# A graph network on one core: other plans for the sparse products, matmuls issued in pairs of groups, pads left out of the first sorting steps, and the W_hh products made ahead

## The chip, the core and the metric

The kernel runs on one core of a Trainium2 chip. The core has a matrix engine (TensorE, PE in the profile; its weight loads are listed as PEld), a vector engine (VectorE, DVE), a scalar engine (ScalarE, ACT), a general engine (GpSimd, POOL) and a queue that only issues transfers (SyncE, SP). Each engine works through its own queue in order and waits on semaphores for the others. The metric is the time of one execution on the device in microseconds (us); a smaller number is better. Differences of 0.3% and less can't be told from no change here.

## The reference

There are N = 12500 nodes with H = 128 features, E = 200000 edges (src, dst) with 16 attributes and a type from 0 to 8. Four message layers follow each other. The first is a gated recurrent layer (GRU), and the other three are graph isomorphism layers (GIN) over the same edges in the other direction:

```
# layer 0: GRU
msg = x[src] @ W_msg.T + b_msg + edge_embed[type]
m   = segment_sum(msg, dst, N)
gi  = m @ W_ih.T + b_ih ;  gh = x @ W_hh.T + b_hh
r, z = sigmoid(gi_r + gh_r), sigmoid(gi_z + gh_z)
n   = tanh(gi_n + r * gh_n)
x   = layernorm(x + (1 - z) * n + z * x)
# layers 1 to 3: GIN, with self loops, ei[0] = src, ei[1] = dst
ee  = edge_attr @ enc_w + enc_b
agg = segment_sum(h[dst] (and ee beside or added), src, N)
h   = relu(bn(agg @ w1 + b1)) @ w2 + b2      (relu after layers 1 and 2)
out = layernorm(x + h)
```

## The kernel before

**Blocks and slots.** The nodes are cut into 98 blocks of 128. A message layer computes, for each of the 98 output blocks, the sum of the rows that its edges name. The edges of an output block come in two forms. For the first `ic` input blocks, the edges of each pair (output block, input block) have 32 slots (`SL`); four such pairs fill a *cell tile* of 128 slots. The edges to the remaining input blocks are packed without regard to their block into `rt` *row tiles* of 128 edges; the last `OV` places of the last row tile also take edges that don't fit into 32 slots. A `Plan` (L31 to 48) holds these numbers: plan C (layer 1) has `ic` = 72 and `rt` = 5, plan D (layers 2 and 3) has `ic` = 60 and `rt` = 7. Layer 0 has cells alone: 25 tiles for 98 blocks.

**One output block in `layer`.** The input table is kept on chip in bf16 as three pieces per number (`X`, 384 columns per block). A cell tile takes four matmuls with 32 columns of weights each (L1550): one-hot weights `g`, made from the row `inr`, pick 32 rows out of each of four input blocks into PSUM. Three tiles make a group (`TG`). ScalarE, in layer 0 for every other group together with VectorE, casts the group from PSUM into `e` (L1556, L1557, L1559). One matmul per tile with the one-hot weights `st` (s in the profile) then adds the 128 slots into the sums of the output block (`scatter`, L1507, the PSUM tile acc). A row tile needs no such step: GpSimd fetches its 128 rows from the table in memory with one indirect DMA (`fetch`, L1484, tile x), and one matmul adds them (`scatter_rows`, L1515). VectorE builds `g` (L1471) and `s` in four pieces (L1474) one block ahead. `finish` adds the three pieces of acc into `s` with three VectorE instructions (L1527 to L1529). Every two blocks a generator does the dense part: `gru` in layer 0 and `gin` in the others; it is advanced by `tick` once per group and yields between steps that wait for each other. All dense steps share one PSUM tile, d.

**Edge attributes.** The generator `attributes` (L729) sums each block's edge attributes. Per block, GpSimd issues 17 indirect DMAs (L736, tile eat), then `add_up` splits, builds one-hots and adds with 17 matmuls (L764). It is advanced during the second sort, in layer 0 (`pace`: k = 1 and 5, and k = 3 in four blocks of five) and in layer 1 (k = 3).

**Before the layers.** Two bitonic sorts of 128x2048 keys run on VectorE, B and then A (`sorter`; L316, L317, L321, L322); 1600 columns hold keys and the others hold pads. Keys are transposed on TensorE and copied back by ScalarE (`turn`). A histogram (`Sizes`, L548, L557, L567) is counted beside sort B. During sort A the kernel also does the attributes' first blocks, the weights (`load_weights`) and the first table (`first_table`). After it, the sorted keys go to memory, and GpSimd gathers the slots of layer 0 from there (`runs`, L791, tile cells); `Slots.decode` turns them into `inrow`, `outcol` and `typecol`.

**Order.** In the sorts the order of VectorE, ScalarE and TensorE is that of the program text (`manual_schedule`). In the layers a scheduler orders every engine's instructions by its own estimates of when each becomes ready.

## Time and profile before

Three runs took 5763.25 to 5779.61 us, with a median of 5772.15 us. The profiled execution took 5775.41 us; its span from the first to the last instruction is 5773.6 us.

| stage, us from the start of the span | length | PE busy | DVE busy | ACT busy | POOL busy | indirect DMAs for attributes (L736) and rows (L1484) |
|---|---|---|---|---|---|---|
| 572 to 1197, sort A and its end | 625 | 167.08 | 476.78 | 104.91 | 500.66 | 405 and 0 |
| 1279 to 2836, layer 0 | 1557 | 1411.98 | 1158.89 | 996.93 | 1073.81 | 935 and 0 |
| 2836 to 3949, layer 1 | 1113 | 999.81 | 492.97 | 739.88 | 821.18 | 323 and 499 |
| 3949 to 4874, layer 2 | 925 | 832.56 | 400.23 | 611.55 | 686.63 | 0 and 685 |
| 4874 to 5774, layer 3 | 900 | 827.81 | 428.78 | 579.76 | 674.90 | 0 and 680 |

The times of the stages' starts are those of the first matmul L1550 of a layer or of the first row fetch L1484 (layer 1). In the profile "busy" is the union of an engine's instructions. For GpSimd the issue of one indirect DMA counts as an instruction, and the time between two issues does not count as busy. In a line of the timeline, the first number is the start, the second the length, "x3" a run of three equal instructions, and the bracket says how long the engine had been idle and what ended that.

### The profile page before, as it was taken

What the parts mean: (1) busy time and instruction counts of PE and PEld (TensorE: products, weight loads), DVE (VectorE), ACT (ScalarE), POOL (GpSimd) and SP (SyncE); (2) the same over time, 40 slices, a digit from 0 to 9 for tenths busy, and PEclk for the clock granted to TensorE, in tenths of its full rate; (3) what the DMA queues carried; (4) which work ended last, traced back from release to release, by engine and by line L of the source; (5) the groups of instructions that cost most, each with busy time, mean ns of one, the idle gap of its engine ahead of it and who ended that gap; (6) DMA issues with size and microseconds to landing.
All of it is one profiled execution on the core that took longest, in us unless ns stands there. A gap on an engine that the chain in (4) does not pass through costs nothing. (4 is left out here: it accounts for less than half of the span.)

```text
span 5773.6 us, 117175 instructions
## 1 busy us (share of the span) xinstructions
PE 4590.5 (80%) x45358; PEld 2754.9 (48%) x45358; DVE 3500.1 (61%) x9502; ACT 3396.2 (59%) x4901; POOL 3855.7 (67%) x3716
## 2 busy tenths in 40 slices
PE   3874252118999999999799989988999997999998
PEld 3774122104444444444355555554555554555555
DVE  9987679837887777777444444443444443444444
ACT  7772131106666666666566666665666665666665
POOL 1001878866676767766677777775777776777776
PEclk9755555559999999999899999999999998999999
DMA  5101130012333333323444444445555555555554
GB/s 65 38 1 33 47 90 7 7 35 74 102 89 86 89 89 101 89 85 89 144 128 125 134 121 129 127 115 166 157 160 158 159 155 167 156 156 156 156 157 131
DMA packets 539973, 616.43 MB, mean 107 GB/s; under 512 B 130184, under 2 KB 458028, under 8 KB 538760
## 3 DMA queue, kind: packets, MB, share of 16 engines
q1 hardware_dynamic: 327302, 373.36, 20.1%
q0 software_dynamic: 148192, 202.82, 14.3%
q10 hardware_dynamic: 63914, 32.71, 2.7%
q8 instruction: 355, 5.82, 0.4%
q14 instruction: 210, 1.72, 0.1%
HBM read 519.72 MB, written 88.82 MB: 105 GB/s over the span
## 5 line engine op out<-in xcount | busy, mean ns | idle before, releaser
L1559 ACT CAST e<-g 128x1152 bf16<-128x1152 f32 (+1 forms) x2058 | 2216.2, 1091 | 907.7 <-PE g L1550 766.3
L1484 POOL DMA_INDIRECT x<-table,rowcol x1862 | 1861.2, 1000 | 641.4 <-issue 600.5
L736 POOL DMA_INDIRECT eat<-in_ea,eidcol x1666 | 1794.8, 1077 | 640.0 <-issue 495.0
L1550 PE MATMUL g<-x,g 128*32 128x384 bf16 x28420 | 1688.1, 333 | 93.6 <-DVE e L1557 54.2
L1507 PE MATMUL acc<-e,s 128*128 128x384 bf16 (+2 forms) x7154 | 1646.8, 344 | 116.9 <-ACT e L1556 51.6
L1507 PEld LDWEIGHTS <-s 128*128 128x128 bf16 (+1 forms) x7154 | 939.2, 153 | 745.4 <-issue 470.4
L1550 PEld LDWEIGHTS <-g 128*32 128x32 bf16 x28420 | 613.0, 96 | 911.6 <-issue 711.1
L1474 DVE TENSOR_TENSOR s<-iotas,outcol 128x704 bf16<-128x704 bf16 (+2 forms) x1568 | 838.7, 544 | 0.3 <-PE acc L1507 0.3
L1471 DVE TENSOR_SCALAR g<-inr,pidx 128x1920 bf16<-128x1920 bf16 (+2 forms) x392 | 329.9, 842 | 793.9 <-PE g L1550 685.7
L1515 PE MATMUL acc<-x,s 128*128 128x384 bf16 x1862 | 512.4, 335 | 155.5 <-DMA x<-table,rowcol 153.9
L1556 ACT CAST e<-g 128x768 bf16<-128x768 f32 x392 | 317.2, 809 | 192.9 <-PE g L1550 126.6
L567 PE MATMUL acc<-ot,oa 125*98 125x101 bf16 x1600 | 295.7, 358 | 126.8 <-ACT ot L548 95.6
L1527 DVE TENSOR_TENSOR s<-s,acc 128x128 f32<-128x128 f32 x392 | 112.5, 287 | 408.5 <-PE acc L1507 402.7
L1515 PEld LDWEIGHTS <-s 128*128 128x128 bf16 x1862 | 271.8, 146 | 176.1 <-issue 147.5
L567 PEld LDWEIGHTS <-oa 125*98 125x98 bf16 x1600 | 292.1, 277 | 129.6 <-issue 87.5
L548 ACT ACTIVATE ot<-dbb,bias 125x160 bf16<-125x160 bf16 (+2 forms) x1078 | 332.4, 406 | 16.4 <-PE acc L567 8.2
L800 POOL IOTA num<- 98x2176 uint16 x1 | 1.9, 1947 | 462.4 <-DMA sortedB<-keyB 462.4
L1427 ACT ACTIVATE gates<-d,shift,scale 128x256 f32<-128x256 f32 x294 | 150.1, 561 | 245.7 <-PE d L1425 245.7
L1557 DVE CAST e<-g 128x384 bf16<-128x384 f32 x392 | 216.6, 553 | 75.2 <-ACT e L1556 70.8
L1440 DVE TENSOR_TENSOR n<-d,b 128x256 f32<-128x256 f32 x98 | 41.6, 424 | 279.7 <-PE d L1435 278.6
L764 PEld LDWEIGHTS <-eoh 128*128 128x128 bf16 x1666 | 116.8, 163 | 197.3 <-DVE eoh L758 172.2
L316 DVE TENSOR_TENSOR keyA<-keyA 128x1024 f32<-128x1024 f32 (+1 forms) x178 | 190.9, 1072 | 15.4 <-ACT keyA L332 12.8
(423 smaller groups left out, 4761.8 us busy)
## 6 DMA issues: line engine op xcount, KB each, us to landing
inr<-inrow SPq DMA_DIRECT2D x196, 480.0 KB
inr<-inrow SPq DMA_DIRECT2D x98, 784.0 KB
inr<-inrow SPq DMA_DIRECT2D x98, 576.0 KB
x<-table,rowcol POOLq DMA_INDIRECT x1862
table<-x SPq DMA_DIRECT2D x147, 192.0 KB
eat<-in_ea,eidcol POOLq DMA_INDIRECT x1666
s<-ovf SPq DMA_DIRECT2D x147, 128.0 KB
ovf<-n SPq DMA_DIRECT2D x98, 128.0 KB
```

The source lines that it names most:

```text
L548: A.activation(self.ot[j % 2][:, b, :ENDS[j] - c0], dbb[:, c0:ENDS[j]], AF.Sign, bias=self.bias[:, b:b + 1], scale=-1.0)
L567: T.matmul(cps[:NB, :NB + NQ - 1], self.oa[c // HC][:, :, c % HC], self.ot[j % 2][:, :, c - (ENDS[j - 1] if j else 0)], start=(c == 0), st ...
L736: G.indirect_dma_start(out=at[:, t, :], out_offset=None, in_=ea, in_offset=bass.IndirectOffsetOnAxis(ap=eidcol[:, b, t:t + 1], axis=0))
L1471: V.tensor_scalar(g[:, :nb * SL], inr[:, :nb * SL], pidx, None, op0=OP.is_equal)
L1474: V.tensor_tensor(st[:, f0:f0 + P // 4, :], iotas[:, f0:f0 + P // 4, :tw], outcol[a][:, o, None, c0:c0 + tw].to_broadcast([P, P // 4, tw]) ...
L1484: G.indirect_dma_start(out=t[:, j, :], out_offset=None, in_=tables[i], in_offset=bass.IndirectOffsetOnAxis(ap=rowcol[:, o, p.kept + j:p.ke ...
L1507: T.matmul(sums[o][:, :wid], st[:m, :, cell + t], e[:m, j, :wid], start=(t == 0), stop=(t == tiles - 1), skip_group_check=True)
L1515: T.matmul(sums[o][:, :H3], st[:, :, row + j], fetched[o][:, j, :], start=False, stop=False, skip_group_check=True)
L1550: T.matmul(pg[c * SL:(c + 1) * SL, j, :H3], g[:, b * SL:(b + 1) * SL], piece(X, b), start=True, stop=True)
L1556: A.copy(e[:, :2, :H3], pg[:, :2, :H3])
L1557: V.tensor_copy(e[:, 2, :H3], pg[:, 2, :H3])
L1559: A.copy(e[:m, :n, :H3], pg[:m, :n, :H3])
```

## The change

1. **Plans.** C has `ic` = 84 and `rt` = 3, D has `ic` = 72 and `rt` = 5; `OV` is 12. A block of layer 1 has 21 cell tiles and 3 row tiles (18 and 5 before), a block of layers 2 and 3 has 18 and 5 (15 and 7 before). The row tiles fetched ahead use all of the X tiles that the table doesn't need, one piece each (`spare`).
2. **The order in `layer`.** TensorE's order is written by hand. Two groups' gathers are issued one after the other, and then the two groups before them are added up (`adding`, `picked`); `tick`, the one-hots' pieces and the attributes' steps are advanced there. `e` has 4 buffers instead of 3. In layers 1 to 3 the groups with odd k are now cast by ScalarE (two tiles) and VectorE (one tile). `finish` uses one reduction over the three pieces of acc and one addition.
3. **W_hh.** A new generator `states` runs after `first_table` during sort A: for each pair of blocks it multiplies x with W_hh, adds b_hn and stores the 3H columns in a memory tensor `hx`. `gru` loads `hx` instead of xT, drops the matmul with W_hh, and adds `hx` to the gates on VectorE. The table `ew` shrinks from 4H to 3H columns. The constants `before`, `nidentb` and `whh` move to a pool that is freed before the layers.
4. **Sorts.** In the merges of runs of 2^k the exchange covers `wide` columns: 1600 for k up to 6, 1664 for k = 7, 1792 for k = 8 and 2048 above.
5. **Attributes.** The steps in sort A end 34 plan entries before its end (20 before); `pace` in layer 0 is k = 1, 3 and 5 in every block; eat has 5 buffers (4 before). The gather of the third chunk of slots stands after the listing.

```
-IC = 72
-CELL = 7
-PLANS = (Plan("C", IC, 5, False, CELL + IC // 4), Plan("D", 60, CELL, True, 0))
+IC = 84
+CELL = 5
+PLANS = (Plan("C", IC, 3, False, CELL + IC // 4), Plan("D", 72, CELL, True, 0))
...
-OV = 8
+OV = 12
...
         def exchange(c, first, cd, halved=False):
+            wide = min(SC, -(-EC // (1 << k)) << k)
...
-                exchanged(bufs[cur], bufs[1 - cur], c, first, cd)
+                exchanged(bufs[cur][:, :wide], bufs[1 - cur][:, :wide], c, first, cd)
...
+    def states():
+        with tc.tile_pool(name="states", bufs=2, side="right") as sp:
+            def load(b0):
+                xt = sp.tile([P, 2 * P], F32, name="xt")
...
+                nc.scalar.dma_start(xt[:, :c1], xT[:, b0 * P:b0 * P + c1])
+                return xt
+            xt = load(0)
+            yield
+            for b0 in range(0, NB, 2):
+                then = load(b0 + 2) if b0 + 2 < NB else None
+                hx = sp.tile([P, 2, 3 * H], F32, name="hxs")
+                for k in range(2):
+                    ps = pss.tile([P, 512], F32, name="split")
+                    T.matmul(ps[:, 0:3 * H], xt[:, k * P:(k + 1) * P], w["whh"], start=True, stop=False,
+                             skip_group_check=True)
+                    T.matmul(ps[:, 2 * H:3 * H], ones[0:1, :], w["bhn"], start=False, stop=True, skip_group_check=True)
+                    A.copy(hx[:, k, :], ps[:, 0:3 * H])
+                nc.sync.dma_start(hxd[b0 * P:(b0 + 2) * P, :].rearrange("(b p) f -> p b f", p=P), hx)
+                yield
+                xt = then
...
-    eap = ctx.enter_context(tc.tile_pool(name="attrs", bufs=4))
+    eap = ctx.enter_context(tc.tile_pool(name="attrs", bufs=5))
...
-        later = chain(load_weights(), first_table())
+        later = chain(load_weights(), first_table(), states())
...
-            if at % 6 if at < len(plan) - 20 else done % ATTR:
+            if at % 6 if at < len(plan) - 34 else done % ATTR:
...
     def gru(i, b0, s):
...
-        nc.sync.dma_start(xt[:, :c1], xT[:, b0 * P:b0 * P + c1])
+        hx = dq.tile([P, 2, 3 * H], F32, name="hx")
+        nc.sync.dma_start(hx, hxd[b0 * P:(b0 + 2) * P, :].rearrange("(b p) f -> p b f", p=P))
...
-            T.matmul(pg, cT[:, ks], w["ew"], start=True, stop=False, skip_group_check=True)
-            T.matmul(pg[:, 0:3 * H], sT[:, ks], w["wa"], start=False, stop=False, skip_group_check=True)
-            T.matmul(pg[:, H:], xt[:, ks], w["whh"], start=False, stop=True, skip_group_check=True)
-            A.activation(gates[:, k, :], pg[:, H:3 * H], AF.Sigmoid)
-            V.tensor_mul(n[:, k, :], gates[:, k, 0:H], pg[:, 3 * H:])
+            T.matmul(pg[:, 0:3 * H], cT[:, ks], w["ew"], start=True, stop=False, skip_group_check=True)
+            T.matmul(pg[:, 0:3 * H], sT[:, ks], w["wa"], start=False, stop=True, skip_group_check=True)
+            V.tensor_add(gates[:, k, :], pg[:, H:3 * H], hx[:, k, 0:2 * H])
+            A.activation(gates[:, k, :], gates[:, k, :], AF.Sigmoid)
+            V.tensor_mul(n[:, k, :], gates[:, k, 0:H], hx[:, k, 2 * H:])
...
+        def add_group(o, st, e, k):
+            if k == 0:
+                sums[o] = psa.tile([P, 512], F32, name="acc")
+            if k == groups - 1:
+                scatter_rows(o, st, 2 * k - 2, rt)
             for j in range(min(TG, tiles - TG * k)):
                 t = TG * k + j
                 m = P if t < NTL - 1 else P // 2
                 T.matmul(sums[o][:, :wid], st[:m, :, cell + t], e[:m, j, :wid], start=(t == 0),
                          stop=(t == tiles - 1), skip_group_check=True)
...
+            if 0 < k < groups - 1:
+                scatter_rows(o, st, 2 * k - 2, 2 * k)
+            if k == groups - 1:
+                finish(o)
...
-            V.tensor_add(so[:, :H], so[:, :H], acc[:, 0:H])
-            V.tensor_add(so[:, :H], so[:, :H], acc[:, H:2 * H])
-            V.tensor_add(so[:, :H], so[:, :H], acc[:, 2 * H:H3])
+            whole = dq.tile([P, H], F32, name="whole")
+            V.tensor_reduce(whole, acc[:, :H3].rearrange("p (k f) -> p f k", k=3), axis=AX.X, op=OP.add)
...
+            V.tensor_add(so[:, :H], so[:, :H], whole)
...
-                if cells_only and n == TG and k % 2 == 0:
+                if n == TG and k % 2 != cells_only:
                     A.copy(e[:, :2, :H3], pg[:, :2, :H3])
                     V.tensor_copy(e[:, 2, :H3], pg[:, 2, :H3])
...
+                picked.append((o, st, e, k))
+                if k % 2 or k == groups - 1:
+                    work += fresh
+                    fresh.clear()
+                    for added_up in adding:
+                        ks = added_up[3]
+                        add_group(*added_up)
+                        tick()
+                        next(pieces, None)
...
+                        if pace(o, ks):
+                            next(attr, None)
+                    if k < 2:
+                        fetch(o + rb - 1)
+                    adding, picked = picked, []
...
-        layer(i, (lambda o, k: k in (1, 5) or k == 3 and o % 5, lambda o, k: k == 3)[i] if i < 2
-              else lambda o, k: False)
+        with tc.tile_pool(name="edges", bufs=4) as ep, tc.manual_schedule(engines={EN.PE}):
+            layer(i, (lambda o, k: k in (1, 3, 5), lambda o, k: k == 3)[i] if i < 2
+                  else lambda o, k: False, ep)
```

## The prediction

> **What bounds the kernel now.** I read the page's engine shares, then the busy time by stage (the table above), the groups of layer 2 and of layer 0 by form, the timeline of a few blocks, and the end of sort A. TensorE is busiest in every layer (832.56 of 925 us in layer 2), but is not what the layers wait for. The groups of layer 2, by form:
>
> ```profile
> L1484 POOL DMA_INDIRECT x<-table,rowcol x685 | 687.6, 1004 | 238.7 <-issue 226.8 <-PE g L1550 6.1 <-DMA x<-table,rowcol 5.2
> L1559 ACT CAST e<-g 128x1152 bf16<-128x1152 f32 x489 | 542.5, 1120 | 222.9 <-PE g L1550 176.3 <-PE d L1435 30.6 <-PE acc L1507 11.0
> L1474 DVE TENSOR_TENSOR s<-iotas,outcol 128x704 bf16<-128x704 bf16 x392 | 199.1, 518 | 0.0
> ```
>
> GpSimd issues 685 row fetches of 1.004 us and sits 0.30 us "issue" between two: 1.30 us each, seven per block, 9.1 us of the 9.2 us that a block takes (900 us from the first gather at 3949.6 to the last at 4849.6, over 98). GpSimd sets layers 2 and 3. In layer 1 it is as full: 822 issues by 1.30 are 1069 of 1113 us. TensorE's own price is read from the timeline of layer 2:
>
> ```profile
> 4401.39 0.67 PE L1550 MATMUL g<-x,g 128*32 128x384 bf16 x12
> 4402.00 0.71 PE L1507 MATMUL acc<-e,s 128*128 128x384 bf16 x3
> 4402.55 0.49 PE L1515 MATMUL acc<-x,s 128*128 128x384 bf16 x2
> 4402.96 0.67 PE L1550 MATMUL g<-x,g 128*32 128x384 bf16 x12
> ...
> 4410.90 0.67 PE L1550 MATMUL g<-x,g 128*32 128x384 bf16 x12
> ...
> 4411.68 1.12 ACT L1559 CAST e<-g 128x1152 bf16<-128x1152 f32 x1 [1.63 <-PE g L1550]
> ...
> 4415.56 1.16 PE L1550 MATMUL g<-x,g 128*32 128x384 bf16 x24
> ...
> 4416.33 2.14 ACT L1559 CAST e<-g 128x1152 bf16<-128x1152 f32 x2 [0.40 <-PE g L1550]
> ...
> 4417.33 1.14 PE L1507 MATMUL acc<-e,s 128*128 128x384 bf16 x6
> ```
>
> The last matmul of a run is shown 0.33 us long, so six tiles' gathers (x24) follow at (1.16-0.33)/5 = 0.166 us each, six additions at 0.162. A run of 12 gathers takes 0.61 us to the next kind, 0.11 more than three tiles; back to gathers costs (0.41-0.32) 0.09. So a cell tile costs 0.33, a row tile 0.16, a change there and back 0.2. ScalarE's cast starts 0.78 us after a group's first gather (4410.90 to 4411.68), and two casts in a row take 1.07 each.
>
> Layer 0, by form: GpSimd takes (962.3+282.3)/925 = 1.345 us per fetch of attributes; the casts follow.
>
> ```profile
> L736 POOL DMA_INDIRECT eat<-in_ea,eidcol x925 | 962.3, 1040 | 409.9 <-issue 282.3 <-DVE attr L757 49.6 <-DVE own L725 18.1
> L1556 ACT CAST e<-g 128x768 bf16<-128x768 f32 x388 | 314.0, 809 | 146.3 <-PE g L1550 123.6 <-DVE s L1474 8.1 <-PE acc L1507 3.0
> L1557 DVE CAST e<-g 128x384 bf16<-128x384 f32 x388 | 214.4, 553 | 73.4 <-ACT e L1556 69.0
> ```
>
> Where a group is shared, VectorE's cast waits for ScalarE's: one after the other. The end of sort A, from the timeline of GpSimd and of VectorE:
>
> ```profile
> 1195.60 0.94 POOL L736 DMA_INDIRECT eat<-in_ea,eidcol  x1 [0.30 <-issue]
> 1196.85 0.98 POOL L791 DMA_INDIRECT cells<-sortedA,start  x1 [0.31 <-issue]
> ...
> 1203.14 0.23 DVE L1093 TENSOR_SCALAR fi<-cells 98x128 int32<-98x128 int32 x1 [38.45 <-DMA cells<-sortedA,start]
> ```
>
> The sort is done at 1162; the slots' gathers stand behind fetches of attributes until 1196.85, and VectorE waits 38.45 us.
>
> **The change, part by part.** The order in which the changed kernel is built gives counts: attributes' fetches 391 in the sort (408 before), 1003 up to layer 1 (935), 272 after (323); runs of gathers in layers 0 to 3: 489, 392, 293, 295 (931, 531, 392, 413).
>
> *Sorts, -40.* Narrow exchanges save 21 x 21.9% + 7 x 18.75% + 8 x 12.5% = 6.9 whole ones of 2 x 1.07 us (L316, L317), 14.8 us per sort. In sort B VectorE is busy 417 of 440 us and ScalarE's histogram keeps pace, so I take 13. GpSimd then starts its attributes (567.4) 13 us earlier and needs (1196.85-567.36)/408 = 1.543 us per fetch: 391 end at 567-13+603 = 1157, 40 us earlier. The gather of the third chunk, moved behind the listing, is built in front of it all the same: four gathers, 5 us at most either way, 0. VectorE's own end (1162-13, less up to 15) and the store of the keys (4 us, as after sort B: 505.9 to 509.9) lie before that. Ends: 0, if something else holds the gathers, and -60.
>
> *W_hh in the sort, 0.* 98 matmuls, casts of 128x384 (0.40 to 0.53 us by L477's 0.533 for 512 columns, at most 52 us), 49 loads on ACT's queue and 49 stores of 384 KB on SP's. ScalarE is busy 105 of the 625 us, TensorE 167, the transfers' share is 0.16: they cover it. Without cover it would hold a turn of the keys: 49 steps by 1 us, +50; below nothing only by a warmer TensorE clock (0.52 here) for the turns, -10. SP's other work there is small; the sums' loads behind it are not needed at once.
>
> *Layer 0, -36.* TensorE loses L1387 (81.3 us), a quarter of L1385's 38.1 and (931-489) x 0.2 = 88 us, some 180 of 1412. VectorE gains 98 additions of the gates (0.424 by L1440, 42 us) and trades three additions (0.84) for a reduction (0.5, between a cast of as many numbers, 0.553, and 2048 columns in 2.28 us, 0.43) and an addition (0.28). All this is hidden by GpSimd: 1003 attribute fetches and 86 others by 1.345 are 1465 us, with 20 of waits 1485, against 1521 now (1315, its first fetch, to 2836, the first row fetch of layer 1). Now it waits 143 us in gaps over 1 us for attributes' buffers and slots; a fifth buffer and a faster TensorE take most of these. If the waits stay at 143 it is +87; if TensorE set the layer, -180. The `hx` loads (384 KB for 128) stand before the one-hots' rows on SP; the DMA share of 0.33 leaves room.
>
> *Layers 2 and 3, 0.* GpSimd falls to 5 x 1.30 = 6.5 us per block. TensorE by rows: 18 x 0.33 + 5 x 0.16 + 3 x 0.2 + the dense part (0.4 transposes, 1.18 for L1424 and L1425, 1.0 for L1435 per two blocks, 1.3 per block) = 8.6. But odd groups are now cast by both engines: 0.78 us to the even group's cast, 1.07 for it, then 0.81 and 0.553 one after the other: 3.21 us from a run's first gather until TensorE may write the odd group's PSUM buffer again. It wants to 0.49 us (three tiles) into the next run. This is the wait that the change adds; behind it on TensorE stand the second gathers, the additions of the two groups before and the dense matmuls, all in a fixed order now, and ScalarE and VectorE wait for these gathers in turn. The six runs of two blocks last 2.17, 2.89, 3.84, 3.17, 2.49, 2.66 us by the prices above. After the first the wait is 3.21-0.49-2.17 = 0.55; in the block without dense work VectorE's cast stands behind the four s pieces (2 us), 0.6 more. 17.2 + 1.2 is 18.4, 9.2 per block: what it takes today. Ends: 8.6 (-59 per layer) and 10.2, if a cast waits behind s pieces twice more (+98). I take 9.2, as the built order shows the waits.
>
> *Layer 1, -19.* 21 x 0.33 + 3 x 0.16 + 4 x 0.2 + 1.3 + attributes 0.3 = 9.8; the run after a single group lasts 1.7, so its wait is 3.21-0.49-1.7 = 1.0; 10.9 against 11.07 now (1085 us of gathers over 98). Ends: 9.8 and 11.9, by the same reasons as in layer 2; GpSimd needs 272 + 294 fetches of 1.30 us, 736 us, and is out of the way. The moved constants and the wider `OV` (four single fetches more by 1.3 us, in layer 0's count) change nothing else.
>
> *Sum.* 5775.41 - 40 - 36 - 19 = 5680 us; the profiled execution is 3 us above the median of 5772.15, which is left in.
>
> [...] If casting set the layers, three more tiles by 1.12/3 in 294 blocks would make an estimated 330 us more, 6010. The row says that ScalarE has room (3 x 1.12 + 3 x 0.81 + 1.0 = 6.8 of 9.2 us).
>
> **Rivals.** *Slower, by VectorE's queue (0.22).* The place is the odd groups' cast in layers 1 to 3: it waits for ScalarE and stands in one queue with s pieces, g (0.755 us and a fifth more) and the reduction, and TensorE's fixed order can't pass a stall. L1557's 69.0 us of waiting for ScalarE speak for it; VectorE's 400 of 925 us busy against. From 0.32 us per block over my 9.2 and 10.9 (95/294) the change is slower; at 1.0 us it is +294, 5970. *TensorE's bare sum (0.13).* The waits close up: -59, -59 and 98 x (11.07-9.8) = -124 with the first two terms: 5775-76-59-59-124 = 5457. For it: fetches leave the path; against: the chain of 3.21 us. *Front terms don't come (0.08).* The sort's end waits for something else and layer 0 keeps its gaps: 5755, no change.
>
> **How the numbers follow.** My case has 0.57, its own range 5600 to 5750. With the rivals the range is 5480 to 5860, which leaves out under 0.1 on each side. About 0.3% (17 us) can't be told from no change: faster 0.69, same 0.08, slower 0.23.
>
> **What would show it.** The gathers L791 start near 1157; the first row fetch of layer 1 near 2760, with GpSimd's gaps of more than 1 us under 40 us in layer 0; row fetches wait in layers 2 and 3, and TensorE's idle time before L1550 is put down to VectorE's cast, some 0.6 us per block. The forecast is wrong if a block of layer 2 takes 8.6 or 10 us, if ScalarE waits for stores in the sort, or if attributes starve TensorE in layer 0.

## The result, and the profile after

The changed kernel takes 5822.15 us (median of four runs, 5818.2 to 5826.93) beside 5774.33 us (four runs too, 5763.25 to 5779.61) for the kernel before: a ratio of 1.0086, with a 95% interval of 1.0068 to 1.0103. It is slower by 48 us, where I had forecast 5680. The profiled execution took 5821.3 us, with a span of 5819.5.

Eleven of the experiments' runs fell on chips that ran the kernel before itself at 8298 to 8577 us; they are kept apart below, and all else compares runs beside a kernel before of 5773 to 5780 us.

The stages show where the time went. The bounds are the first fetch of attributes in layer 0 (L771; before L736), the first row fetch of layer 1 (L1526; before L1484), the first gather matmul of layers 2 and 3 (L1597; before L1550), and the end of the span. For layers 2 and 3 they lie earlier than the stages of the table in front, at 3915.1 and 4847.2 in the kernel before instead of 3949 and 4874, since a layer's first gathers run before the last steps of the layer before it. All in us; "off by" is what came less what was forecast.

| stage | before | forecast | after | off by |
|---|---|---|---|---|
| up to the first fetch of layer 0 | 1315.2 | -40 | 1283.9 (-31) | +9 |
| layer 0 | 1521.0 | -36 | 1579.8 (+59) | +95 |
| layer 1 | 1078.9 | -19 | 1113.4 (+34) | +53 |
| layer 2 | 932.1 | 0 | 920.8 (-11) | -11 |
| layer 3 to the end | 926.4 | 0 | 921.6 (-5) | -5 |

The five differences add up to +46, that of the two spans. The sorts did what was said. The end of sort A, from the timelines of GpSimd and VectorE (start, length, engine, line, and in brackets the idle time before it and what ended that):

```profile
1156.44 0.94 POOL L771 DMA_INDIRECT eat<-in_ea,eidcol  x1 [0.31 <-issue]
1157.69 0.99 POOL L829 DMA_INDIRECT cells<-sortedA,start  x1 [0.31 <-issue]
...
1163.98 0.23 DVE L1132 TENSOR_SCALAR fi<-cells 98x128 int32<-98x128 int32 x1 [14.69 <-DMA cells<-sortedA,start]
```

The slots' gathers start at 1157.69 (1157 was forecast, 1196.85 before), and VectorE waits 14.69 us there instead of 38.45.

Layer 0 became longer. Its groups by form: engine, tiles and shapes, count, then busy time and mean ns, then idle time before and what ended it.

```profile
L771 POOL DMA_INDIRECT eat<-in_ea,eidcol x1003 | 1062.3, 1059 | 422.4 <-issue 294.7 <-DVE attr L792 64.4 <-DVE e L1609 29.7
L1597 PE MATMUL g<-x,g 128*32 128x384 bf16 x9548 | 526.7, 345 | 96.2 <-DVE e L1604 82.3 <-ACT e L1606 10.3
L1604 DVE CAST e<-g 128x384 bf16<-128x384 f32 x389 | 214.8, 552 | 124.9 <-ACT e L1603 121.5
```

GpSimd issues 1079 gathers from the first fetch to the first row fetch, busy for 1143 us with 325 us of gaps under 1 us, so 1.36 us each (1.345 were forecast); its gaps over 1 us come to 108 us, where I had forecast under 40 (159 in the kernel before, by the same count).

Layer 2, by form:

```profile
L1526 POOL DMA_INDIRECT x<-table,rowcol x490 | 474.8, 969 | 473.2 <-PE acc L1548 182.5 <-issue 151.7 <-PE d L1455 100.0
L1597 PE MATMUL g<-x,g 128*32 128x384 bf16 x7070 | 361.3, 329 | 42.5 <-DVE e L1604 36.1 <-ACT e L1606 6.2
L1606 ACT CAST e<-g 128x1152 bf16<-128x1152 f32 x294 | 329.0, 1119 | 220.5 <-PE g L1597 214.9 <-DMA table<-x 2.9 <-ACT x L1354 1.7
```

GpSimd now has 473 us of idle time, 152 of them "issue", and waits for the additions (PE acc L1548): it no longer sets the layer. TensorE waits 42.5 us before its gathers. A block takes 9.4 us, of which TensorE is busy for 8.84 and idle for 0.56.

In layer 1 the wait that the forecast named is plain in the timeline, at the run behind a single group:

```profile
3421.70 1.16 PE L1597 MATMUL g<-x,g 128*32 128x384 bf16 x24
3422.42 1.12 ACT L1606 CAST e<-g 128x1152 bf16<-128x1152 f32 x1 [0.56 <-PE g L1597]
3423.43 0.81 ACT L1603 CAST e<-g 128x768 bf16<-128x768 f32 x1
3423.53 0.56 DVE L1574 TENSOR_REDUCE whole<-acc 128x128 f32<-128x384 f32 x1 [1.93 <-PE acc L1559]
3423.59 0.67 PE L1597 MATMUL g<-x,g 128*32 128x384 bf16 x12
3424.01 0.58 DVE L1517 TENSOR_TENSOR s<-iotas,outcol 128x832 bf16<-128x832 bf16 x1
3424.51 0.55 DVE L1604 CAST e<-g 128x384 bf16<-128x384 f32 x1
3425.11 0.67 PE L1597 MATMUL g<-x,g 128*32 128x384 bf16 x12 [0.85 <-DVE e L1604]
```

The odd group's buffer is free 3.41 us after the run's first gather (3421.70 to 3425.11; I had 3.21). In the last 0.27 of that, VectorE is still at the reduction and one s piece, which stand before the cast in its queue: ScalarE ended at 3424.24, the cast began at 3424.51. TensorE idles 0.85 us and, with everything behind it in the written order, waits.

### The profile page after: what moved, and what is told of

Read it like the earlier page. It is cut to its first block, busy times and chain, and to the rows that moved or that the text cites. A ratio compares the mean times of both kernels' runs of the same rounds, so it can differ in the third digit from the quotient of the medians.

```text
span 5819.5 us, 127038 instructions
## 1 busy us (share of the span) xinstructions
PE 4662.1 (80%) x49380; PEld 3043.0 (52%) x49380; DVE 4006.1 (69%) x10052; ACT 3441.4 (59%) x5288; POOL 3284.7 (56%) x3132
## 5 line engine op out<-in xcount | busy, mean ns | idle before, releaser
L771 POOL DMA_INDIRECT eat<-in_ea,eidcol x1666 | 1828.8, 1098 | 682.0 <-issue 477.3
L1606 ACT CAST e<-g 128x1152 bf16<-128x1152 f32 (+1 forms) x1470 | 1583.2, 1077 | 783.5 <-PE g L1597 728.1
L1526 POOL DMA_INDIRECT x<-table,rowcol x1274 | 1255.4, 985 | 1233.6 <-PE acc L1548 498.7
L1597 PE MATMUL g<-x,g 128*32 128x384 bf16 x31948 | 1678.3, 334 | 307.3 <-DVE e L1604 236.0
L1559 PE MATMUL acc<-e,s 128*128 128x384 bf16 (+1 forms) x8036 | 1756.0, 346 | 2.2 <-DVE e L1609 1.4
L1559 PEld LDWEIGHTS <-s 128*128 128x128 bf16 x8036 | 1069.0, 152 | 589.1 <-issue 467.7
L1597 PEld LDWEIGHTS <-g 128*32 128x32 bf16 x31948 | 778.4, 97 | 1027.3 <-issue 740.3
L1603 ACT CAST e<-g 128x768 bf16<-128x768 f32 x1274 | 1023.6, 803 | 367.4 <-PE g L1597 258.7
L1604 DVE CAST e<-g 128x384 bf16<-128x384 f32 x1274 | 703.5, 552 | 456.2 <-ACT e L1603 428.6
L1517 DVE TENSOR_TENSOR s<-iotas,outcol 128x832 bf16<-128x832 bf16 (+1 forms) x1568 | 831.5, 566 | 0.0
L1574 DVE TENSOR_REDUCE whole<-acc 128x128 f32<-128x384 f32 x392 | 217.4, 555 | 545.4 <-PE acc L1559 545.4
L1514 DVE TENSOR_SCALAR g<-inr,pidx 128x2304 bf16<-128x2304 bf16 (+2 forms) x392 | 356.3, 909 | 167.4 <-PE g L1597 165.5
L1548 PE MATMUL acc<-x,s 128*128 128x384 bf16 x1274 | 335.0, 325 | 0.5 <-DMA x<-table,rowcol 0.4
L1548 PEld LDWEIGHTS <-s 128*128 128x128 bf16 x1274 | 188.3, 148 | 21.0 <-issue 1.4
L323 DVE TENSOR_TENSOR keyA<-keyA 128x1024 f32<-128x1024 f32 (+4 forms) x178 | 185.3, 1041 | 17.7 <-ACT keyA L339 14.9
L799 PEld LDWEIGHTS <-eoh 128*128 128x128 bf16 x1666 | 116.9, 162 | 131.3 <-DVE eoh L793 49.4
L324 DVE TENSOR_TENSOR keyA<-keyA 128x1024 f32<-128x1024 f32 (+4 forms) x178 | 184.5, 1037 | 0.0
```

What stands on the lines that cost most here:

```text
L771: G.indirect_dma_start(out=at[:, t, :], out_offset=None, in_=ea, in_offset=bass.IndirectOffsetOnAxis(ap=eidcol[:, b, t:t + 1], axis=0))
L1514: V.tensor_scalar(g[:, :nb * SL], inr[:, :nb * SL], pidx, None, op0=OP.is_equal)
L1517: V.tensor_tensor(st[:, f0:f0 + P // 4, :], iotas[:, f0:f0 + P // 4, :tw], outcol[a][:, o, None, c0:c0 + tw].to_broadcast([P, P // 4, tw]) ...
L1526: G.indirect_dma_start(out=fetched(o, j), out_offset=None, in_=tables[i], in_offset=bass.IndirectOffsetOnAxis(ap=rowcol[:, o, p.kept + j:p ...
L1548: T.matmul(sums[o][:, :H3], st[:, :, row + j], fetched(o, j), start=False, stop=False, skip_group_check=True)
L1559: T.matmul(sums[o][:, :wid], st[:m, :, cell + t], e[:m, j, :wid], start=(t == 0), stop=(t == tiles - 1), skip_group_check=True)
```

## The experiments

Each kernel is the changed one with the edit shown ("..." marks what is left out of one). "Ratio" is to the kernel before, run beside it on the same chip; stages as above, taken from each kernel's trace.

| kernel | median us | ratio, 95% interval | layer 0 | layer 1 | layer 2 | layer 3 |
|---|---|---|---|---|---|---|
| after_again | 5827.31 | 1.0082 [1.0066, 1.0099] | 1580.4 | 1116.4 | 920.6 | 923.2 |
| pace_half_2 | 5887.70 | 1.0188 [1.0171, 1.0205] | 1600.3 | 1148.3 | 920.9 | 924.9 |
| whole_casts_2 | 5702.78 | 0.9862 [0.9846, 0.9879] | 1580.8 | 1062.8 | 883.6 | 887.1 |
| free_l0_c | 5604.00 | 0.9707 [0.9691, 0.9724] | 1487.3 | 1065.2 | 884.3 | 887.7 |
| free_pace | 5562.40 | 0.9638 [0.9622, 0.9654] | 1420.8 | 1089.1 | 884.3 | 887.5 |
| free_half | 5495.57 | 0.9505 [0.9489, 0.9521] | 1345.5 | 1098.1 | 881.9 | 887.6 |
| free_plans_b | 5723.47 | 0.9906 [0.9890, 0.9923] | 1501.3 | 1060.1 | 930.8 | 940.6 |

**Does GpSimd set layer 0? (pace_half_2)** The forecast said so. The test moves attributes' fetches from layer 0 to layer 1, so that 833 instead of 1003 are left.

```
-            layer(i, (lambda o, k: k in (1, 3, 5), lambda o, k: k == 3)[i] if i < 2
+            layer(i, (lambda o, k: k in (1, 5) or k == 3 and o % 2, lambda o, k: k == 3 or k == 5 and o % 2)[i] if i < 2
```

> The changed kernel itself, as the yardstick for the kernels of this call. In the call before, the kernel before took 8577 us and every engine had long idle times with its inputs there, ScalarE for example 17.25 us at once; where the kernel before takes 5770 again, this one takes 5820, ratio 1.009. Where it takes 8580 again, this one lies near the two kernels of that call that differ least from it, 7640 to 7700, ratio 0.89 to 0.90.

> Fewer attributes in layer 0 (833 fetches instead of 1003), more in layer 1, once more. Theory A, GpSimd sets layer 0: the first row fetch near 2670 instead of 2864, layer 1 longer by 22: 5650. Theory B, TensorE's written order with its waits sets it: 5820 to 5845.

Layer 0 took 1600 us, 20 more, with 170 fetches fewer. Theory A falls, and with it the forecast's reason for this layer. Theory B is right about the direction, but the time, 5887.70, is 43 us above its range. TensorE idles as long in layer 0 as in after_again (304 and 305 us). Its busy time is 21 us longer although ten blocks of attributes have left the layer, and its work at half the granted clock (shown further down) is 261 us instead of 189. Layer 1 took 32 us more, where 22 were expected. The waits of pace_half_2 in layer 0 (engine and line, what it waited for, us in total, times, longest):

```profile
POOL eat L771 <- DVE e L1609: 238.6, 38, 12.2
...
PEld L812 <- DVE n L1429: 108.8, 48, 2.8
```

GpSimd now waits for the rest: its gaps over 1 us rise from 101 to 327 us. And TensorE waits 48 times, once in every two blocks, at L812, the transposition of an attributes' block, for `gru` (L1429) to give the tile d back.

**The shared casts (whole_casts_2).**

```
-                if n == TG and k % 2 != cells_only:
+                if cells_only and n == TG and k % 2 == 0:
```

> The odd groups' casts of layers 1 to 3 by ScalarE alone, once more. Theory C, the shared cast frees the PSUM buffer late (3.36 us after a run's first gather, by ScalarE alone 2.93): layer 1 -40, layers 2 and 3 -17 each: 5750. Rival, ScalarE's dense work then stands before casts: 5830 to 5900. In the call before, a block of layer 2 took 10.31 us with whole casts and 10.98 to 11.00 in the other three kernels, which speaks for theory C, though there all engines had idle times of another kind.

It is 124.5 us faster than after_again, more than theory C's 74, and lies where C put it: layer 1 loses 53.6, layers 2 and 3 37.0 and 36.1, layer 0 nothing. The same place of layer 1 in its timeline:

```profile
3425.07 1.16 PE L1597 MATMUL g<-x,g 128*32 128x384 bf16 x24
3425.85 4.19 ACT L1606 CAST e<-g 128x1152 bf16<-128x1152 f32 x4 [0.61 <-PE g L1597]
3426.16 0.71 PE L1559 MATMUL acc<-e,s 128*128 128x384 bf16 x3
3427.02 0.67 PE L1597 MATMUL g<-x,g 128*32 128x384 bf16 x12
3428.04 0.67 PE L1597 MATMUL g<-x,g 128*32 128x384 bf16 x12 [0.35 <-ACT e L1606]
```

The buffer is free after 2.97 us instead of 3.41, and TensorE waits 0.35 instead of 0.85. The sums over a layer say the same. These are TensorE's gathers in layer 1 of the changed kernel, in layer 1 of this one, and in layer 2 of this one (those of layer 2 in the changed kernel are shown above, with 42.5 us of idle time):

```profile
L1597 PE MATMUL g<-x,g 128*32 128x384 bf16 x8208 | 425.6, 329 | 116.9 <-DVE e L1604 83.4 <-ACT e L1606 24.1
L1597 PE MATMUL g<-x,g 128*32 128x384 bf16 x8208 | 425.4, 329 | 72.5 <-ACT e L1606 58.6
L1597 PE MATMUL g<-x,g 128*32 128x384 bf16 x7051 | 354.4, 329 | 9.7 <-ACT e L1606 6.6 <-DMA x<-table 2.9
```

So 44 of the 54 us in layer 1 and 33 of the 37 in layer 2 are waits of TensorE for its buffers. The edit does two things: it ends the wait of one cast for the other, and it takes 294 casts of 0.55 us per layer out of VectorE's queue. two_tiles (further down) was meant to part them, but ran only beside a kernel before of 8577 us, so that stays open. The rival (ScalarE as the new bound) is out: with all casts it was busy for 633 us with these casts in layer 2's 880, and waited 94 us for gathers.

**TensorE's written order in layer 0 (free_l0_c).** If GpSimd does not set layer 0, the waits in TensorE's order might. In the changed kernel's layer 0 (its timeline, cut to the lines that matter):

```profile
1881.66 0.91 PE L1425 MATMUL d<-wa,sT 128*128 128x384 f32 x2
1882.61 0.42 DVE L1426 TENSOR_TENSOR gates<-d,hx 128x256 f32<-128x256 f32 x1 [1.26 <-PE d L1425]
1883.07 0.42 ACT L1427 ACTIVATE gates<-gates 128x256 f32<-128x256 f32 x1 [1.13 <-DVE gates L1426]
1883.52 0.29 DVE L1428 TENSOR_TENSOR n<-gates,hx 128x128 f32<-128x128 f32 x1 [0.48 <-ACT gates L1427]
1883.85 0.29 DVE L1429 TENSOR_TENSOR n<-n,d 128x128 f32<-128x128 f32 x1
1884.19 1.24 PE L799 MATMUL d<-attr,eoh 128*128 128x49 bf16 x17 [1.61 <-DVE n L1429]
1885.36 1.74 PE L1597 MATMUL g<-x,g 128*32 128x384 bf16 x24
...
1887.04 2.19 PE L1559 MATMUL acc<-e,s 128*128 128x394 bf16 x6
```

The attributes' matmuls (L799) need d, which `gru` holds until L1429. The written order puts them in front of the gathers, so TensorE stands for 1.61 us. What follows is slow as well: six additions take 2.19 us here, and 1.23 or 1.24 in 304 of the layer's 358 runs of six. The same moments by stretches (length, busy us of PE, PEld, DVE, ACT, POOL with instructions, granted TensorE clock, DMA share, GB/s):

```profile
1881.00:1884.10 3.10, 1.57 (x6) 0.50 (x4) 1.33 (x5) 1.36 (x2) 2.49 (x3) 1.00 0.08 8
1884.10:1885.30 1.20, 1.11 (x17) 1.11 (x17) 0.03 (x1) 0.00 (x0) 0.90 (x2) 1.00 0.09 7
1885.30:1889.20 3.90, 3.90 (x34) 1.60 (x32) 3.06 (x11) 2.37 (x4) 2.98 (x4) 0.56 0.05 6
1889.20:1892.60 3.40, 1.79 (x8) 0.76 (x8) 2.00 (x8) 1.43 (x5) 2.49 (x4) 1.00 0.08 8
1892.60:1896.00 3.40, 3.40 (x26) 1.46 (x29) 2.68 (x7) 0.76 (x2) 2.79 (x3) 0.50 0.82 241
```

After both stretches with such a hole the granted clock is half (a mean of 0.56 and 0.50 in the stretches behind them). In layer 0 of the changed kernel 52 half-clock stretches begin, 46 of them 3.41 us long, 235 us in all, in which TensorE was busy for 195 us and so lost an estimated 97, half of that; in the kernel before there are 8, and it lost 19. TensorE's idle times over 0.7 us add up to 248 us from the first fetch to the first row fetch, against 71 before. Of these, 166 us (103 times) stand in front of matmuls that write the tile d, against 13 us (8 times) before.

```
-        with tc.tile_pool(name="edges", bufs=4) as ep, tc.manual_schedule(engines={EN.PE}):
+        with tc.tile_pool(name="edges", bufs=4) as ep, (tc.manual_schedule(engines={EN.PE}) if i else ExitStack()):
```

This and the kernels that follow have whole casts in layers 1 to 3 too, so this one stands against whole_casts_2; those after it keep this edit and stand against it.

> Whole casts in layers 1 to 3 (5703 us beside a kernel before of 5780) and, in layer 0 alone, TensorE's order left to the scheduler; a third time. Theory D (steps that need the tile d or VectorE's pieces wait in front of the gathers, 150 us, and the clock granted behind such waits is half, 97 us of work against 27 before): layer 0 falls to GpSimd's floor of 1515 us from 1580: 5640 to 5660, with TensorE's idle times over 0.7 us near 90 us and the half-clock stretches near 80 us. Rival E, VectorE's queue holds layer 0 up: 5690 to 5715. Rival F, 931 changes of kind again: 5720 to 5790.

Layer 0 falls by 93.5 us and the time by 98.8 (90 by the two ratios, as the two ran on different chips): theory D, with more than it promised (the floor that I had put at 1515 was 1487). TensorE's idle times over 0.7 us are 107 us, 30 of them in front of matmuls that write d; its half-clock stretches are 13, with 32 us lost. The runs of gathers (gathers with no other matmul between) rise from 489 to 650, which by 0.2 us each costs 32 us of TensorE's time; the forecast priced these changes of kind, and they were the smaller matter. GpSimd's gaps over 1 us in this layer are now 2.5 us in all, and it is the bound: 1079 gathers of 1.37 us.

```profile
L771 POOL DMA_INDIRECT eat<-in_ea,eidcol x1003 | 1070.0, 1067 | 312.0 <-issue 286.2 <-DMA eat<-in_ea,eidcol 7.6 <-DVE e L1609 6.0
```

With TensorE's order free the scheduler also orders VectorE, ScalarE and GpSimd anew, so the run shows that the written order is the cause, with all that hangs on it, but does not part the two halves, the idle times and the half clock.

**What GpSimd then sets (free_pace, free_half).** The same kernel with 935 fetches in layer 0 (`pace` as in the kernel before) and with 833 (as in pace_half_2).

> The kernel free_l0 with the old pace of the attributes in layer 0 (935 fetches instead of 1003 there, 340 instead of 272 in layer 1). If theory D holds and GpSimd sets layer 0 once TensorE's order is free, 68 fetches by 1.36 come off it, -92, down to TensorE's own limit (13.1 us of matmuls per block, 1284): layer 0 1430 to 1450; layer 1 gets four blocks of attributes more, +9: 5560 to 5580. If TensorE or VectorE still sets layer 0, the same time as free_l0 and 9 us more.

> The kernel free_l0 with 833 fetches of attributes in layer 0 and 442 in layer 1 (free_l0: 1003 and 272, 5604 us; free_pace: 935 and 340, 5562 us). In free_pace GpSimd issues 1008 gathers in layer 0 at 1.38 us each with 23 us of waits, but TensorE's last gather there is at 2625 and the first row fetch at 2697. Theory A now (GpSimd sets layer 0 once TensorE's order is free): 1276 + 909 x 1.38 = 2530, which TensorE can't follow; its own end, 2625 in free_pace, is the floor, so the first row fetch comes at 2610 to 2640: -60 to -85, and layer 1 pays ten blocks of attributes by 2.2 less what its waits for GpSimd hide: 5490 to 5525. Rival: TensorE or VectorE sets layer 0 already in free_pace and the attributes only move: 5555 to 5580.

Layer 0 falls by 66.5 and 141.8 us against free_l0_c. In free_half 909 gathers at 1.40 us and 44 us of longer waits are 1315 of the 1345 us; TensorE's last gather there is at 2597 and the first row fetch at 2626, 29 us later (98 in free_l0_c, where TensorE had little left to do while the attributes' fetches were still being issued). Layer 1 pays 24 and 33 us. The pace that cost 60 us in the written order (pace_half_2 against after_again) brings 108 in the free one. free_half, 5495.57 us, beats both kernels: 0.9505 of the time before.

**The plans by themselves (free_plans_b).**

```
-IC = 84
-CELL = 5
-PLANS = (Plan("C", IC, 3, False, CELL + IC // 4), Plan("D", 72, CELL, True, 0))
+IC = 72
+CELL = 7
+PLANS = (Plan("C", IC, 5, False, CELL + IC // 4), Plan("D", 60, CELL, True, 0))
-OV = 12
+OV = 8
```

> The kernel free_l0 (5604 us; layer 1 from the first row fetch to its last gather 1064 us, layers 2 and 3 881 and 872 us) with the plans of the kernel before (72 and 60 input blocks in cells, 5 and 7 row tiles). Layer 1: three cell tiles by 0.33 and a run by 0.2 fewer, two rows by 0.16 more, -0.87 per block, -85, down to 980 to 1000, where GpSimd's 762 issues by 1.30 (990) would set it. Layers 2 and 3: GpSimd's 7 x 1.30 and 0.1, 9.2 per block, are 900 each, +20 and +28. Sum 5565 to 5590: then the new plans cost in layer 1 what they bring in layers 2 and 3. Rival G: GpSimd, full in layer 1, holds rows back behind attributes' fetches: layer 1 stays at 1064 or above, and the time is 5650 or more: then the new plans are a gain everywhere.

The time is far from the 5565 to 5590 expected. Layers 2 and 3 take 930.8 and 940.6 us, about what they took in the kernel before (932.1 and 926.4): with seven row tiles GpSimd sets them. In layer 2 its 686 issues of 1.305 us are 895 of the 931 us. Layer 2 by form:

```profile
L1526 POOL DMA_INDIRECT x<-table,rowcol x686 | 686.5, 1001 | 279.9 <-issue 155.9 <-PE acc L1548 33.2 <-PE g L1597 32.3
...
L1548 PE MATMUL acc<-x,s 128*128 128x384 bf16 x686 | 187.8, 333 | 53.1 <-DMA x<-table,rowcol 53.0
```

The additions of rows wait 53 us for the rows. In layer 1 the old plan is no shorter (1060 against 1065): GpSimd issues its 762 gathers within 1014 us of that stage, with 8 us of longer waits, and sets that layer too. So rival G has the time right (5650 or more), and half of the reason: no gain in layer 1, but no loss either. Layer 0 is 14 us longer here than in free_l0_c, with 18 us of GpSimd's gaps over 1 us instead of 2.5; where they come from stays open. The new plans are worth 47 us in layer 2 and 53 in layer 3, once the casts are whole.

**Runs beside a kernel before of 8298 to 8577 us.** These were four chips; one of them gave the kernel before 8577 us and, at another time, 5780. In whole_casts (beside 8577), and in free_l0 and plans_before_whole (beside 8312), ScalarE and VectorE had long idle times with nothing in the trace to wait for: in whole_casts VectorE's at L1514 and L1609 come to 305.4 and 268.8 us. Waits of ScalarE there ("remote" is a releaser that the trace doesn't know), and one of them in the timeline:

```profile
ACT e L1606 <- remote: 670.9, 123, 20.1
...
ACT e L1603 <- remote: 503.6, 52, 17.7
```

```profile
2066.35 0.80 ACT L1603 CAST e<-g 128x768 bf16<-128x768 f32 x1 [17.25 <-remote]
```

The gathers that this cast reads had ended by 2050.1. What the runs gave:

| kernel before | kernels and ratios |
|---|---|
| 8576.67 | pace_as_before 0.8941, pace_half 0.8876, whole_casts 0.8759, two_tiles 0.8907 |
| 8312.03 | free_l0 0.8694, attr_first 0.8858, plans_before_whole 0.9680 |
| 8320.11 | free_plans 0.9508, attr_first_2 0.8854 |
| 8298.53 | free_l0_b 0.8719, attr_first_b 0.8875 |

Four of these kernels have no run elsewhere: the old pace in the written order (pace_as_before, free_pace's pace without its other edits); the two halves of a shared cast in two tiles (two_tiles); whole casts with the attributes' step of layer 0 moved (attr_first); and whole casts with the plans of free_plans_b (plans_before_whole). Excerpts of the two edits that are shown nowhere else:

```
# two_tiles
-                    A.copy(e[:, :2, :H3], pg[:, :2, :H3])
-                    V.tensor_copy(e[:, 2, :H3], pg[:, 2, :H3])
+                    A.copy(e01[:, :, :H3], pg[:, :2, :H3])
+                    V.tensor_copy(e2[:, :H3], pg[:, 2, :H3])
...
# attr_first
+                    for added_up in adding if cells_only else ():
+                        if pace(o, added_up[3]):
+                            next(attr, None)
                     for added_up in adding:
...
-                        if pace(o, ks):
+                        if not cells_only and pace(o, ks):
```

> The changed kernel with the old pace of the attributes in layer 0 (k = 1 and 5, and k = 3 in four blocks of five): 935 instead of 1003 fetches of attributes before the first row fetch. Theory A, GpSimd sets layer 0: in the changed kernel it issues 1079 gathers there at (1143 + 325) / 1079 = 1.36 us and waits 120 us. 68 fetches fewer are 92 us: the first row fetch moves from 2864 to about 2771; layer 1 gets 68 fetches more (634 issues by 1.30 are 824 of 1155 us, hidden) and four blocks of attributes on TensorE by 2.2 us, 9 us. Time 5740. Theory B, TensorE's written order sets layer 0 (its casts' waits and the wait for the tile d): GpSimd just follows, the first row fetch moves by less than 20 us and the time stays over 5800.

> The changed kernel with the shared casts written to two tiles (ScalarE's two in one, VectorE's one in another), so that neither has to wait for the other. Theory C: the odd group's buffer is free 0.72 + 1.12 + 0.81 = 2.65 us after a run's first gather, 0.7 before the 3.36 of now: layer 1 loses most of its 0.9 us of waits per block, -70, layers 2 and 3 0.5 us per two blocks, -25 each. Layer 0 has the shared group first: its waits (91 us for VectorE's cast) close up, but nothing is gained there if GpSimd sets it (theory A); if TensorE sets it (theory B), -90. Time 5700 with A, 5610 with B. Rival: VectorE's cast now waits at the head of its queue for the gathers and holds back the pieces of s behind it: no gain in layers 1 to 3, 5800 or more.

> Whole casts in layers 1 to 3 (5703 us); TensorE's order stays written out, but in layer 0 the attributes' step is issued straight behind the two groups' gathers instead of behind the dense step that has just taken the tile d. Theory D: of the 1.6 us that L799 and L812 wait for d, the two gathers cover 1.0: the idle times behind L1425 (37 of 1.62 us) shrink to some 0.6, -38, and with them go about 26 of the 52 half-clock stretches, each 1.7 us: -44. The floor by GpSimd is 65 under today. Time 5635 to 5665. Rival E, VectorE's queue: no change, 5690 to 5715; a new wait may come in front of the additions: up to 5760.

> Whole casts in layers 1 to 3 (5703 us), with the plans of the kernel before (72 and 60 input blocks in cells, 5 and 7 row tiles). Layer 1 loses three cell tiles by 0.33 and one run by 0.2 and gets two rows by 0.16: -0.87 per block, -85, unless GpSimd sets it: 490 + 272 issues by 1.30 are 990 us, under the 1107 - 85 = 1022 then left. Layers 2 and 3: GpSimd's 7 x 1.30 = 9.1 and 0.1 are 9.2 per block against 8.98 and 8.90 now: +22 and +29. Sum 5669. Rival G: GpSimd, then full in layer 1, holds rows back behind attributes' fetches: layer 1 stays at 1090 and more, and the time is 5735.

> Whole casts in layers 1 to 3 (5703 us); TensorE's order written out, but in layer 0 the attributes' step stands straight behind the two groups' gathers. Theory D: the idle times behind L1425 (37 of 1.62 us) shrink to some 0.6, -38, and with them about 26 of the 52 half-clock stretches of 1.7 us, -44; GpSimd's floor is 65 under today: 5635 to 5665. Rival E, VectorE's queue: 5690 to 5715; a new wait in front of the additions: up to 5760.

> Whole casts in layers 1 to 3 (5703 us); TensorE's order written out, but in layer 0 the attributes' step stands straight behind the two groups' gathers; once more. Theory D: the 37 idle times of 1.62 us behind L1425 shrink to some 0.6, -38, and with them about 26 of the 52 half-clock stretches of 1.7 us, -44; GpSimd's floor is 65 under today: 5635 to 5665. Rival E, VectorE's queue: 5690 to 5715. Against D: where the kernel before took 8312 and 8320, GpSimd waited 17 times for VectorE's L761 in this kernel, a wait that the others don't have; then 5700 to 5760.

The others are kernels shown above, on such chips (free_l0 and free_l0_b are free_l0_c, free_plans is free_plans_b):

> The changed kernel with still fewer attributes in layer 0 (k = 1 and 5, and k = 3 in odd blocks: 833 fetches) and more in layer 1 (k = 3, and k = 5 in odd blocks). Theory A: 170 fetches fewer in layer 0 are 231 us, until TensorE with its waits sets it; its matmuls without waits take 13.1 us per block there, so I expect a floor of about 14 per block: the first row fetch near 2670. Layer 1: 442 + 294 issues by 1.30 are 957 us, hidden, and ten blocks of attributes by 2.2 us more, 22. Time 5650. Theory B: no gain in layer 0, layer 1 longer by 22: 5820 to 5845.

> The changed kernel with the odd groups' casts of layers 1 to 3 by ScalarE alone, as before. Theory C, the shared cast (ScalarE, then VectorE) frees the odd group's PSUM buffer late: from a run's first gather 0.72 + 1.12 + 0.81 + 0.55 = 3.20 us, 3.36 as the timeline of layer 1 shows it; by ScalarE alone 0.72 + 1.12 + 1.09 = 2.93. The waits of 0.87 and 0.99 us per block in layer 1 and of 0.50 us per two blocks in layers 2 and 3 shrink by 0.3 to 0.43 each: layer 1 -40, layers 2 and 3 -17 each, layer 0 unchanged: 5750. Rival, ScalarE then becomes the bound: 7 x 1.10 + 0.9 of dense work is 8.6 of 11.3 us per block in layer 1 and 6 x 1.12 + 0.9 = 7.6 of 9.3 in layers 2 and 3, so it has room on average, but where dense work stands before a cast the gathers wait for it: 5830 to 5900.

> Whole casts in layers 1 to 3 (5703 us) and, in layer 0 alone, TensorE's order left to the scheduler. Pace_half showed that GpSimd doesn't set layer 0: 170 fetches fewer left it as long. Theory D: in the written order the steps that need the tile d or VectorE's pieces (L799, L812, the second L1411) stand in front of the gathers and wait there 1.5 to 1.8 us, 18 or 19 times each, some 150 of the 236 us of TensorE's idle times over 0.7 us (90 us before); and behind such a wait the granted clock falls to 0.5 for 3.41 us: 52 such stretches, 97 us of TensorE's work lost (27 before). Without the written order both go back toward the old figures, and layer 0 falls until GpSimd sets it: 1079 x 1.36 = 1468 and its waits at both ends, 47, are 1515 against 1580 now. Time 5640 to 5660. Rival E: VectorE's queue holds up layer 0, whatever TensorE's order: no change, 5690 to 5715. Rival F: the scheduler's order brings back the 931 changes of kind by 0.2 us (+88): 5720 to 5790.

> Whole casts in layers 1 to 3 (5703 us) and, in layer 0 alone, TensorE's order left to the scheduler; once more, beside a kernel before that should take 5770 to 5780 here. Theory D (steps that need the tile d or VectorE's pieces wait in front of the gathers, 150 us, and the clock granted behind such waits is half, 97 us of work against 27 before): layer 0 falls to GpSimd's floor of 1515 us from 1580: 5640 to 5660. Rival E, VectorE's queue holds it up: 5690 to 5715. Rival F, 931 changes of kind again: 5720 to 5790. Where the kernel before took 8312, this one's layer 0 took 2525 us and the one with the attributes' step moved 2681, which is for D.

> Three edits that lie in different stages, read stage by stage against whole_casts_2 (5703 us; first row fetch 2868, layer 1's gathers 1107 us, layers 2 and 3 880.5 and 872.6): whole casts in layers 1 to 3; TensorE's order left to the scheduler in layer 0 alone; the plans of the kernel before (72 and 60 input blocks in cells, 5 and 7 row tiles). Layer 0, theory D (in the written order the steps that need the tile d or VectorE's pieces wait in front of the gathers, 150 us, and the clock granted behind such waits is half, 97 us of work against 27 before): layer 0 falls to GpSimd's floor, 1468 + 47 = 1515 from its first fetch, first row fetch 2800 to 2815. Rival E, VectorE's queue holds it up: 2860 and later. Rival F, 931 changes of kind again: later than 2880. Layer 1: three cell tiles and a run fewer, two rows more: 1022, if GpSimd's 762 issues by 1.30 (990) leave it; rival G, GpSimd full and rows behind attributes' fetches: 1090 and more. Layers 2 and 3: GpSimd's 9.2 per block, 900 each (+20, +28).

None of the expected times was met, since none was meant for such chips. Where two kernels that ran on one of them can be set beside each other, their order is that of the runs above: whole casts before shared ones, a free order before a written one, the new plans before the old. Beside the kernel before it is another matter: pace_half is 0.8876 here and 1.0188 above, and why it turns round stays open, as does what the engines wait for on these chips. attr_first's layer 0 is longer than that of the free order on both chips that ran both (2681 us from its first gather to its last against 2525 beside 8312). GpSimd waits there 17 times, 261.5 us, at L771 for VectorE's L761, against 2 times and 15.9 us in the free order. So it seems that moving one step by hand moved the wait; the written order without that step was not run on these two chips. Whether two_tiles would beat whole casts where the kernel before takes 5775 was not measured.

## Why the prediction was wrong

**Sorts, -40: right.** The gathers L829 came at 1157.69 for 1157; 391 fetches were in front of them, as counted. Of the 39 us, 31 are left at the first fetch of layer 0.

**W_hh in the sort, 0: right as far as seen.** Nothing in the sort's end came later than forecast. The granted clock from 572 to 1197 was 0.62 (0.52 before), and the turns' matmuls were no shorter for it: 422 ns (L338), 420 before (L331). No run takes this part alone.

**Layer 0, -36: wrong, and the step that failed is "All this is hidden by GpSimd".** In its sum, GpSimd's 1465 us of issues came as 1468, but the 20 us of GpSimd's waits came as 108: GpSimd was held up by the others. I priced TensorE's matmuls (180 us less) and not its order; a layer that TensorE sets even stands there as -180. In the written order one late step holds all that stands behind it: L799 waits 1.61 us for d at 1884.19, and 24 gathers and six additions wait behind it. The layer from its first fetch to the first row fetch, in the kernel before, in the changed one, and in free_l0_c (bounds, length, then busy us of PE, PEld, DVE, ACT and POOL, granted TensorE clock, DMA share, GB/s):

```profile
1315.00:2836.00 1521.00, 1389.11 (x14392) 697.68 (x14393) 1142.90 (x4363) 986.35 (x1454) 1054.21 (x1015) 0.98 0.33 93
1284.00:2864.00 1580.00, 1275.77 (x14332) 722.76 (x14325) 1195.88 (x4374) 973.67 (x1466) 1143.14 (x1080) 0.93 0.35 99
1277.00:2764.00 1487.00, 1260.60 (x14379) 710.64 (x14376) 1174.81 (x4380) 963.88 (x1470) 1153.09 (x1080) 0.94 0.36 105
```

TensorE's busy time fell by 113 us only, as the half clock took back an estimated 78 (97 less 19), and its idle time rose by 172, from 132 to 304. The two make the 59 us by which the layer grew. That is an account and no proof; the proof that the written order is behind it is free_l0_c. There TensorE idles 226 us, 91 of them after its last gather, with GpSimd still at the attributes' fetches. The forecast asked what stands behind a wait in the fixed order, but only for the casts' wait in layers 1 to 3; in layer 0, where the order is written by the same lines and the dense steps and the attributes share the tile d, it did not. Its last part came near the case ("attributes starve TensorE in layer 0"), without a price. A smaller slip: the 143 us that it read as GpSimd's waits in the kernel before are 159, if every gap over 1 us of that stage is counted. Its number for a layer that GpSimd does set was good: first row fetch "near 2760, with GpSimd's gaps of more than 1 us under 40 us" is what free_l0_c shows (2763.9, and 2.5 us).

**Layer 1, -19: wrong by 53.** The wait was named and in the right place: 1.0 us per block behind the single group. Averaged over the layer, TensorE's idle times came to 1.26 us per block, in part since the reduction and an s piece stood before the cast, and its work to 10.1 us instead of 9.8. The rest is the sum itself: its terms, 9.8 and 1.0, make 10.8 and not 10.9, and I compared with 11.07 per block over the gathers, while over the stage a block took 11.0 before and 11.36 after.

**Layers 2 and 3, 0: right** (9.4 per block; 9.2 forecast, 9.5 before by the stages used here). The terms came about as forecast: in layer 2 TensorE worked 8.84 us per block (8.6) and idled 0.56 (0.6). The balance was also that of the forecast: the new plans save about what the shared casts cost. whole_casts_2 and free_plans_b measure both sides, 37 and 36 us for the casts, 47 and 53 for the plans with whole casts.

**The rivals.** "Slower, by VectorE's queue" is what came in layer 1, 0.46 us per block over my value (it said that from 0.32 on the change is slower); layers 2 and 3 were 0.2 over it, and no slower than before. The larger part of the miss, 95 of some 140 us, lies in layer 0, where it saw none. So that the time came out slower, as this rival said, is in the main for another reason than its own. "TensorE's bare sum" had its 8.6 per block for layers 2 and 3; with whole casts they took 9.0.

**The estimate of 6010.** It supposed that casting sets the layers. The kernel that used ScalarE alone in layers 1 to 3 was 124.5 us faster than the one that used ScalarE and VectorE. ScalarE had room: in layer 2 of whole_casts_2 it was busy with all the casts for 633 of 880 us, and a buffer came free 2.97 us after the run's first gather with one engine and 3.41 with two one after the other. The estimate of 6010 was far too high.

## What to carry to other kernels

An order written by hand is a promise that no step in it is ever late. For each step ask when its inputs and its buffer are there, and what stands behind it. Where several generators share one buffer, try the scheduler's order first: here it was worth 94 us in layer 0. Before a copy is split between two engines, ask whether the halves run side by side; where the second waits for the first and stands in a busy queue, the buffer can come free later than with one engine (3.41 us against 2.97 here). A bound that one engine's counts show (here GpSimd's) is only the bound once the others can keep up; a run with less of that engine's work tells.

## What was not expected of the hardware

**Half the clock behind short holes.** The trace of the changed kernel gives the granted TensorE clock in steps of 3.41 us, at 1.0 or 0.5. For the layers of the changed kernel (1284 to 5800) I cut the time into these steps, took TensorE's busy share in each step at the full clock, and counted what clock the next step got:

| busy share of a step | up to 0.44 | 0.5 | 0.6 | 0.7 | 0.8 and more |
|---|---|---|---|---|---|
| next step at full clock | 0 | 10 | 17 | 103 | 1045 |
| next step at half clock | 17 | 31 | 8 | 2 | 0 |

(shares rounded to tenths; the step with the hole of 1.61 us shown above has 0.53). And of the 89 steps at half clock, the 31 with a share of 0.8 or less were all followed by another at half, the 58 with 0.9 or more by a full one. So in this kernel idle time of half a step, some 1.7 us, was mostly enough (31 of 41). It costs the hole and an estimated 1.7 us at most, half of 3.41, of work in the step that follows: behind the hole of 1.61 us six additions took 2.19 us, beside 1.23 or 1.24 in 304 of layer 0's 358 runs of six.
